# First layer of a two-layer cross-attention kernel: one step of the context's turning ahead of tile 0's scores, three ahead of tile 1's

## The chip, the cores and the metric

The kernel runs on one core of a Trainium2 chip. The metric is the time of one execution in microseconds on the device; the profile beside it is of one other execution. The engines are TensorE (PE; PEld is its weight load), VectorE (DVE), ScalarE (ACT), GpSimd (POOL) and SyncE (SP, which issues most DMAs).

## The reference

Two layers run over x (2048 tokens by 256) and a context of 1601 rows by 192. The change lies in the first layer's attention. Cut to that:

```python
tok = input_tokens @ W_proj + b_proj                      # 1601 x 256
scores = einsum('bnd,bsd->bns', prev_states, tok) / sqrt(D)
attn = softmax(scores, axis=-1)
routed = einsum('bns,bsd->bnd', attn, tok)
# then: layer norms, gates u and r, a candidate, new_state = (1-u)*prev + u*cand, a layer norm
```

The second layer is self-attention with 16 heads, cross-attention to the context with 16 heads, and an MLP. All is float32.

## The kernel before

**First layer.** The scores are not made from `tok` but with the projection folded into the queries: `queries(b)` multiplies 512 tokens of x (turned, `xy_sb`) by `wT_sb`, the turned W_proj, and copies the result back into `xy_sb` on ScalarE (L265). `scores(t)` multiplies 128 tokens (a tile, 16 in all) by the context as it comes from memory, features on the partitions (`ctxA` 128 rows, `ctxB` the other 64, held twice). It writes 1601 scores into two PSUM buffers of 801 and 800, first the product with `ctxA` in four pieces, then the one with `ctxB`. VectorE takes the maximum of each half (L302) and forms the shift (L306, L310), with a bias term that `query_bias(t)` has summed (GpSimd L279, ScalarE L280). ScalarE then writes the exponentials of each half into `pr_xn` (L313). `turned(t)` transposes them in 32x32 blocks on VectorE into `pT` (L320).

**The context's turning.** For the values the context is needed with its rows on the partitions. `turn_context(i0, n)` transposes n blocks of 128 context rows on TensorE, two transposes a block (L331 through the helper at L101, and L333), into one PSUM buffer, and ScalarE copies them out two blocks at a time (L341) into `tok_ctx`, which lies in the places of `pT` that tiles 6 and 7 use later. There are 13 blocks, in four calls: (0,4), (4,4), (8,4) and (12,1). `spread_context` then copies `tok_ctx` by 20 DMAs on SyncE's queue (L352, L356) into `ctx4`, which `mean_context(0)` reads after tile 7.

**What sets the order.** `kept` holds each engine's instructions in the order in which the program names them, so the calls' order in the source is the order on TensorE, VectorE, ScalarE and GpSimd. DMAs on SyncE's queue are ordered by a scheduler. PSUM buffers come from `half()`: four buffers of 2 x 512 floats on 128 partitions, taken in turn; one `queries`, one `turn_context` takes one, `scores` takes two. Whoever takes a buffer waits until its last reader is done with it.

The order around the change is: `queries(0)`, `query_bias(0)`, `scores(0)`, two turning steps, `query_bias(1)`, `scores(1)`, `turned(0)`, the other two steps and the spreading, loads of x, `queries(1)`, and then tiles 2 to 7.

**After that** come the remaining queries, `mean_context(0)`, tiles 8 to 15, projections, `mean_context(1)`, the gates with the second layer's preparation interleaved by a written list (`FIRST`), the long stretch of the second layer's attention, and the MLP.

Of the kernel before, what the change touches and what calls it, by code (L numbers as in the profile page):

```python
# [70 lines left out]
def xattn_kernel(  # L71
# [21 lines left out]
    def kept(ins):  # L93
        tc.keep_in_program_order(ins)
        return ins

    def mm(out_, lhsT, rhs, **kw):
        kept(nc.tensor.matmul(out_, lhsT, rhs, **kw))  # L98

    def transpose(out_, in_):  # L100
        kept(nc.tensor.transpose(out_, in_, ident))  # L101
# [39 lines left out]
    def row(name, p=P):  # L141
        at, w = _ROWS[name]
        t, base = rows_of[at < first_rows]
        return t[:p, at - base : at - base + w]
# [89 lines left out]
    def half():  # L234
        return halves.tile([P, 2, QB], F32, name="half")
# [17 lines left out]
    def queries(b):  # L253
        pt = half()
        for m in range(2):
            for c in range(2):
                mm(
                    pt[:, m, :],
                    wT_sb[:, c, m * P : (m + 1) * P],
                    xy_sb[:, c, b * QB : (b + 1) * QB],  # L260
                    start=(c == 0),
                    stop=(c == 1),
                )
        for m in range(2):
            kept(nc.scalar.copy(xy_sb[:, m, b * QB : (b + 1) * QB], pt[:, m, :]))  # L265
# [10 lines left out]
    def query_bias(t):  # L276

        xb = xbs[t % 2]
        kept(nc.gpsimd.tensor_mul(xb, res[:, t, :], row("b_proj")))  # L279
        kept(nc.scalar.activation(xb, xb, AF.Identity, accum_out=cbs[:, t : t + 1]))  # L280

    def scores(t):
        hs = [half().rearrange("p b n -> p (b n)") for _ in range(2)]
        pieces = [hs[0][:, LEFT:], hs[1][:, : L - H0]]
        outs = [pieces[i // 2][:, n0 - (i // 2) * H0 :][:, :nw] for i, (n0, nw) in enumerate(KEYS)]
        tok = slice(t * P, (t + 1) * P)


        for o, (n0, nw) in zip(outs, KEYS):
            mm(  # L290
                o, xy_sb[:, 0, tok], ctxA[:, n0 : n0 + nw],
                start=True, stop=False, skip_group_check=True,
            )
        for i, (o, (n0, nw)) in enumerate(zip(outs, KEYS)):
            r = slice(i % 2 * (C - P), (i % 2 + 1) * (C - P))
            mm(
                o, xy_sb[r, 1, tok], ctxB[r, n0 : n0 + nw],
                start=False, stop=True, skip_group_check=True,
            )
        nm2 = small.tile([P, 2], F32, name="l0_nm2")  # L300
        for i in range(2):
            kept(nc.vector.tensor_reduce(nm2[:, i : i + 1], pieces[i], AX.X, ALU.max, negate=True))  # L302
        nmx = small.tile([P, 1], F32, name="l0_nmx")
        cb = cbs[:, t : t + 1]
        kept(
            nc.vector.scalar_tensor_tensor(  # L306
                nmx, nm2[:, 0:1], nm2[:, 1:2], cb, ALU.min, ALU.subtract
            )
        )
        kept(nc.vector.tensor_scalar(nmx, nmx, cb, 1.0 / 16.0, ALU.add, ALU.mult))  # L310
        for i, (k0, kw) in enumerate(((0, H0), (H0, L - H0))):
            kept(
                nc.scalar.activation(  # L313
                    pr_xn[:, t % 2, k0 : k0 + kw], pieces[i], AF.Exp, bias=nmx, scale=1.0 / 16.0,
                    accum_out=dens[:, t, i : i + 1],
                )
            )

    def turned(t):
        kept(nc.vector.transpose(pT[:, t % T8, :], pr_xn[:, t % 2, :]))  # L320
# [5 lines left out]
    def turn_context(i0, n):  # L326
        pt = half()
        for i in range(n):
            k0, kw = LC[i0 + i]
            at_i = pt[:kw, i // 2, i % 2 * C : (i % 2 + 1) * C]  # L330
            transpose(at_i[:, :P], ctxA[:, k0 : k0 + kw])  # L331
            kept(
                nc.tensor.transpose(  # L333
                    at_i[:, P:], ctxB[: C - P, k0 : k0 + kw], ident[: C - P, : C - P]
                )
            )
        for b in range(0, n, 2):
            m = min(2, n - b)
            kw = LC[i0 + b][1]
            kept(  # L340
                nc.scalar.copy(  # L341
                    tok_ctx[:kw, i0 + b : i0 + b + m, :],
                    pt[:kw, b // 2, : m * C].rearrange("p (i n) -> p i n", n=C),
                )
            )

    def spread_context():
        for j in range(P // HP):
            r = slice(j * HP, (j + 1) * HP)
            n = (KB - 1 - j) // 4 + 1 if j != (KB - 1) % 4 else (KB - 1) // 4  # L350
            for i in range(P // HP):
                nc.sync.dma_start(ctx4[i * HP : (i + 1) * HP, j::4, :][:, :n, :], tok_ctx[r, :n, :])  # L352
        left = L - (KB - 1) * HP
        j = (KB - 1) % 4
        for i in range(P // HP):
            nc.sync.dma_start(  # L356
                ctx4[i * HP : i * HP + left, KB - 1, :],
                tok_ctx[j * HP : j * HP + left, (KB - 1) // 4, :],
            )
# [96 lines left out]


    queries(0)
    query_bias(0)
    scores(0)  # L460
    turn_context(0, 4)
    turn_context(4, 4)
    query_bias(1)
    scores(1)
    turned(0)
    turn_context(8, 4)
    turn_context(12, 1)
    spread_context()
    for t4 in range(2, 4):
        load_x(t4)  # L470
    queries(1)
# [805 lines left out]
```

## Time and profile before

| what | us |
|---|---|
| median of 3 runs (1918.60 to 1924.24) | 1922.65 |
| the profiled execution's own time | 1927.1 |
| its span | 1925.3 |
| TensorE busy in the span | 1909.5 |
| VectorE busy | 1423.1 |
| ScalarE busy | 1339.0 |
| GpSimd busy | 675.6 |

The span is the part of the execution that the profile's records cover; 1.8 us lie around it. The first layer ends at about 196 us of the span. Mean granted clock of TensorE over the span: 0.996. Lines of the profile below give, for a group of instructions, its start, its duration, the engine, the line of the code, the operation, the tile written and the tiles read, the shape, the count, and in brackets the engine's idle time before it and what ended it.

### The profile page before, as it was taken

To read this page: it belongs to the slowest core of one execution; us is meant where nothing else is said; L and a number is where in the kernel's file an instruction comes from. 1 tells how busy PE (TensorE), PEld (TensorE's weight loads), DVE (VectorE), ACT (ScalarE), POOL (GpSimd) and SP (SyncE) were. 2 spreads that over 40 slices of the span, in tenths; PEclk is the share of its full clock that TensorE was granted. 3 is DMA by queue.
4 is the path that set the end of the run, shared out by engine and by line. 5 is a ranking of instruction groups with operands and counts; after the bars stand their busy time and mean duration, and the time that the engine had idled before them with its cause. 6 is when DMAs were issued, how large, how long until landed. Compare 5 with 4: busy or idle time off the path is not lost.

```text
span 1925.3 us, 39186 instructions
## 1 busy us (share of the span) xinstructions
PE 1909.5 (99%) x14774; PEld 855.0 (44%) x14774; DVE 1423.1 (74%) x2546; ACT 1339.0 (70%) x2598; POOL 675.6 (35%) x850
## 2 busy tenths in 40 slices
PE   8999999999999999999999999999999999999999
PEld 4758775433333333433333344333333433443466
DVE  3563575888888888878888888788888878886210
ACT  3322433188887888788888887887888788888621
POOL 1202334034444444343444444344444344343010
PEclk9999998999999999999999999999999999999999
DMA  7400404500000000000000000000000000000000
GB/s 198 96 32 24 51 1 83 81 3 6 6 5 2 5 5 5 8 5 5 5 5 5 5 5 5 5 7 2 27 26 5 8 5 5 5 5 2 1 22 22
DMA packets 32894, 38.27 MB, mean 20 GB/s; under 512 B 12416, under 2 KB 25088, under 8 KB 32320
## 3 DMA queue, kind: packets, MB, share of 16 engines
q1 hardware_dynamic: 30880, 29.98, 7.3%
q0 software_dynamic: 1168, 4.11, 0.8%
q10 hardware_dynamic: 656, 1.67, 0.6%
q8 instruction: 116, 1.90, 0.4%
q14 instruction: 74, 0.61, 0.1%
HBM read 16.27 MB, written 2.62 MB: 10 GB/s over the span
## 4 chain that ended last, share of the span: by engine, by line
PE 85%; DVE 4%; POOL 1%; DMA 0%; issue 0%; ACT 0%; DVEq 0%; POOLq 0%
PE bank L98 84%; DVE mxp L670 2%; PE bank L101 1%; DMA stage<-in_ca_wq_dram 0%; DVE bn_st L827 0%; DVE bn_st L892 0%; DVE nr_v L178 0%; DVE cand_sb L977 0%; DVE res L978 0%; DVE res L995 0%; POOL ca_wo_sb L537 0%; DVE mvb L828 0%; DVE cand_sb L976 0%; POOL rs_o_a L186 0%; DVE res L990 0%
## 5 line engine op out<-in xcount | busy, mean ns | idle before, releaser
L670 DVE TENSOR_REDUCE mxp<-bank 128x1 f32<-128x512 f32 x1792 | 1109.1, 681 | 171.9 <-PE bank L98 165.4
L716 ACT ACTIVATE pt<-bank 128x512 f32<-128x512 f32 (+1 forms) x1856 | 959.8, 602 | 201.3 <-PE bank L98 200.7
L742 POOL TENSOR_TENSOR acc<-acc,part 128x512 f32<-128x512 f32 x414 | 526.0, 1270 | 840.9 <-ACT part L741 840.9
L98 PE MATMUL bank<-qa,k_sa 32*128 32x512 f32 x2048 | 519.7, 615 | 0.4
L98 PE MATMUL bank<-k_sa,qa 32*128 32x512 f32 x2048 | 504.8, 619 | 0.0
L98 PE MATMUL bank<-k_ca,qa 32*128 32x512 f32 (+1 forms) x2048 | 432.6, 531 | 0.0
L98 PE MATMUL bank<-qa,k_ca 32*128 32x512 f32 (+1 forms) x1664 | 414.9, 617 | 0.0
L98 PEld LDWEIGHTS bank<-qa,k_sa 32*128 32x128 f32 x2048 | 216.5, 183 | 226.4 <-DVE mxp L670 203.6
L98 PE MATMUL bank<-pt,v_sa 128*32 128x512 f32 x2048 | 272.8, 605 | 0.0
L741 ACT COPY part<-bank 128x512 f32<-128x512 f32 x414 | 252.7, 610 | 13.2 <-PE bank L98 10.0
L98 PEld LDWEIGHTS bank<-qa,k_ca 32*128 32x128 f32 (+1 forms) x1664 | 166.4, 179 | 179.6 <-DVE mxp L670 143.5
L98 PEld LDWEIGHTS bank<-k_sa,qa 32*128 32x128 f32 x2048 | 197.5, 184 | 69.6 <-ACT pt L716 44.2
L98 PE MATMUL bank<-pt,v_ca 128*32 128x512 f32 (+1 forms) x1664 | 225.0, 605 | 0.0
L98 PEld LDWEIGHTS bank<-k_ca,qa 32*128 32x128 f32 x2048 | 196.4, 184 | 47.3 <-ACT pt L716 32.7
L98 PEld LDWEIGHTS bank<-pt,v_sa 128*32 128x32 f32 x2048 | 40.3, 108 | 192.1 <-ACT pt L716 191.1
L98 PEld LDWEIGHTS bank<-pt,v_ca 128*32 128x32 f32 (+1 forms) x1664 | 34.7, 108 | 150.6 <-ACT pt L716 148.6
L1195 DVE TENSOR_TENSOR o<-bank,res 128x512 f32<-128x512 f32 (+1 forms) x9 | 5.6, 631 | 97.0 <-PE bank L98 97.0
L98 PE MATMUL half<-l_pT,ctx 32*128 32x256 f32 (+1 forms) x1632 | 71.0, 376 | 2.7 <-DVE routed L418 1.3
L98 PE MATMUL half<-ctx_w,xy_sb 128*128 128x512 f32 (+5 forms) x256 | 71.1, 516 | 1.1 <-ACT xy_sb L265 0.7
L98 PEld LDWEIGHTS half<-l_pT,ctx 32*128 32x128 f32 (+1 forms) x1632 | 65.3, 158 | 8.6 <-issue 3.7
L313 ACT ACTIVATE pr_xn<-half,l_nmx 128x801 f32<-128x801 f32 (+1 forms) x32 | 29.4, 925 | 47.5 <-DVE l_nmx L310 47.5
L302 DVE TENSOR_REDUCE l_nm<-half 128x1 f32<-128x801 f32 (+1 forms) x32 | 30.2, 986 | 34.8 <-PE half L98 34.8
(187 smaller groups left out, 1307.6 us busy)
## 6 DMA issues: line engine op xcount, KB each, us to landing
ctx<-l_pT SPq DMA_DIRECT2D x8, 312.0 KB
ctx<-l_pT SPq DMA_DIRECT2D x8, 288.0 KB
xy_sb<-in_xT_dram SPq DMA_DIRECT2D x4, 512.0 KB
res<-in_x_dram SPq DMA_DIRECT2D x4, 512.0 KB
k_sa<-hT_sa SPq DMA_DIRECT2D x16, 128.0 KB
k_sa<-k SPq DMA_DIRECT2D x64, 32.0 KB
qa<-hT_sa SPq DMA_DIRECT2D x64, 32.0 KB
qa<-hT SPq DMA_DIRECT2D x64, 32.0 KB
```

The source lines that it names most:

```text
L98: kept(nc.tensor.matmul(out_, lhsT, rhs, **kw))
L101: kept(nc.tensor.transpose(out_, in_, ident))
L302: kept(nc.vector.tensor_reduce(nm2[:, i : i + 1], pieces[i], AX.X, ALU.max, negate=True))
L313: nc.scalar.activation(pr_xn[:, t % 2, k0 : k0 + kw], pieces[i], AF.Exp, bias=nmx, scale=1.0 / 16.0, accum_out=dens[:, t, i : i + 1],)
L670: kept(nc.vector.tensor_reduce(mxps[n][:, j, qt, kb : kb + 1], mx, AX.X, ALU.max))
L716: kept(nc.scalar.activation(pt[:kw], sc[:kw], AF.Exp, scale=HD**-0.5))
L741: kept(nc.scalar.copy(part, av))
L742: kept(nc.gpsimd.tensor_add(accs[n], accs[n], part))
L1195: kept(nc.vector.tensor_add(o[:, some, :], po[:, :n, :], res[:, t0 : t0 + n, :]))
```

## The change

`turn_context(0, 4)` is moved from behind `scores(0)` to ahead of `query_bias(0)`. The calls `turn_context(8, 4)`, `turn_context(12, 1)` and `spread_context()` are moved from behind `turned(0)` to ahead of `query_bias(1)`. Nothing else differs: every instruction is issued as often as before.

```diff
     queries(0)
+    turn_context(0, 4)
     query_bias(0)
     scores(0)
-    turn_context(0, 4)
     turn_context(4, 4)
+    turn_context(8, 4)
+    turn_context(12, 1)
+    spread_context()
     query_bias(1)
     scores(1)
     turned(0)
-    turn_context(8, 4)
-    turn_context(12, 1)
-    spread_context()
     for t4 in range(2, 4):
         load_x(t4)
     queries(1)
```

The order of the built programs differs on TensorE, ScalarE and SyncE as the diff says, and nowhere behind `queries(1)` on any engine; of the 16 large copies of `spread_context` the first that is issued is one of 13 blocks where it was one of 12.

## Prediction

> **What bounds the kernel now.** I read the page first (busy time of each engine), then the chain of waits, then TensorE's waits over the whole span, then the timeline of TensorE and ScalarE in the first 40 us, and at the end the stretches with their granted clock.
>
> The page:
>
> ```profile
> span 1925.3 us, 39186 instructions
> PE 1909.5 (99%) x14774; PEld 855.0 (44%) x14774; DVE 1423.1 (74%) x2546; ACT 1339.0 (70%) x2598; POOL 675.6 (35%) x850
> PE 85%; DVE 4%; POOL 1%; DMA 0%; issue 0%; ACT 0%; DVEq 0%; POOLq 0%
> ```
>
> TensorE (PE) has work 1909.5 of 1925.3 us, and 85% of the chain that ended last is TensorE. So a change of order gains at most TensorE's holes, about 16 us in all, and one made ahead of tile 1 reaches only the holes that stand there. TensorE's waits, the first of up to 300 us, the second of from 300 us on:
>
> ```profile
> PE half L98 <- ACT xy_sb L265: 1.2, 2, 0.7
> PE half L98 <- ACT pr_xn L313: 0.9, 1, 0.9
> ...
> PE bank L98 <- DVE v_ca L1046: 2.0, 1, 2.0
> ```
>
> The first has two parts, 0.68 us ahead of tile 0's scores and 0.53 at 71 us. The timeline of TensorE shows where they stand (start, duration, idle before in brackets):
>
> ```profile
> 8.03 6.58 PE L98 MATMUL half<-xy_sb,rows_sb 128*128 128x512 f32 x8 [1.93 <-DMA xy_sb<-in_xT_dram]
> 15.29 4.50 PE L98 MATMUL half<-ctx_w,xy_sb 128*128 128x289 f32 x16 [0.68 <-ACT xy_sb L265]
> 19.72 0.33 PE L101 MATMUL half<-ident,ctx_w 128*128 128x128 f32 x1
> ...
> 23.42 4.51 PE L98 MATMUL half<-ctx_w,xy_sb 128*128 128x289 f32 x16
> 27.86 0.33 PE L101 MATMUL half<-ident,ctx_w 128*128 128x128 f32 x1
> ...
> 29.96 0.27 PE L333 MATMUL half<-ident,ctx_w 64*65 64x64 f32 x1
> 31.10 5.30 PE L98 MATMUL half<-xy_sb,rows_sb 128*128 128x512 f32 x8 [0.88 <-ACT pr_xn L313]
> 36.25 26.58 PE L98 MATMUL half<-ctx_w,xy_sb 128*128 128x289 f32 x96
> 62.75 7.13 PE L98 MATMUL half<-xy_sb,rows_sb 128*128 128x512 f32 x16
> ```
>
> The reader is to see five pieces: queries(0) until 14.61; scores(0) at 15.29; two turning steps 19.72 to 23.42 (3.70 us, 1.85 each); scores(1) 23.42 to 27.86; the last two steps until 30.22, then a hole of 0.88, and queries(1) at 31.10. From 36.25 on TensorE runs without a hole to 69.8. The hole of 0.68 is ScalarE's copy of the queries; that of 0.88 is the PSUM buffer of scores(1)'s first half, which queries(1) takes next and which the exponential (L313) gives back.
>
> queries(1) took 36.25 - 31.10 = 5.15 us, while queries(2) and (3) together took 69.82 - 62.75 = 7.07, 3.54 each. The 1.6 us between are the clock, in the table of stretches (third figure from the end: the share of the clock that was granted; behind it DMA share and GB/s):
>
> ```profile
> 30.00:31.00 1.00, 0.23 (x2) 0.09 (x1) 1.00 (x1) 0.97 (x3) 0.00 (x0) 0.98 0.00 0
> 31.00:32.00 1.00, 0.90 (x1) 0.50 (x2) 0.72 (x1) 1.00 (x4) 0.00 (x0) 0.50 0.00 0
> ...
> 34.00:35.00 1.00, 1.00 (x4) 0.40 (x3) 0.00 (x0) 0.00 (x0) 0.00 (x0) 0.82 0.80 159
> ...
> 315.00:317.00 2.00, 2.00 (x7) 0.95 (x10) 2.00 (x5) 0.92 (x2) 2.00 (x4) 0.50 0.26 57
> ```
>
> Half clock from about 31.0 to 34.4 (3.4 us), and again from about 314.3 (0.82 mean in 313 to 315) to 324.5 (0.62 in 323 to 325), 10.2 us, which cost about half of it, 5.1.
>
> **The change, part by part.** No instruction is added or taken away: 26 transposes, 7 ScalarE copies and 20 DMAs issue as before. turn_context(0,4) moves ahead of scores(0); turn_context(8,4), (12,1) and spread_context move ahead of scores(1).
>
> *Step 1, ahead of scores(0).* The context's rows that it reads are there: SyncE's queue reuses the semaphores of those loads, and its waits for them end at 11.30 and 13.1. It needs no copy of the queries, so it starts when queries(0) ends, at 14.61, and takes 1.85: scores(0) starts at 16.46, not 15.29. The 0.68 hole is filled: 1.85 of work costs 1.17. Its two copies (0.40 us each, from four in 1.62) lie in ScalarE's idle 1.79 us ahead of query_bias(0) at 17.51. Gain 0.68.
>
> *Steps 2 to 4, ahead of scores(1).* With t the start of scores(0), from the same trace: TensorE is done with it at t + 4.43, with two turning steps at t + 8.13, and with the 0.52 of turn_context(12,1) at t + 8.65. The four PSUM buffers are taken in turn, so turn_context(12,1) takes tile 0's first half and scores(1) its second. The exponentials say when these are free:
>
> ```profile
> 21.91 0.93 ACT L313 ACTIVATE pr_xn<-half,l_nmx 128x801 f32<-128x801 f32 x1 [3.88 <-DVE l_nmx L310]
> ...
> 22.82 0.92 ACT L313 ACTIVATE pr_xn<-half,l_nmx 128x800 f32<-128x800 f32 x1
> ...
> 23.73 1.62 ACT L341 COPY l_pT<-half 128x384 f32<-128x384 f32 x4
> ```
>
> The first ends at 22.84, t + 7.55, against t + 8.13: 0.58 to spare. The second ends at 23.74, t + 8.45, against t + 8.65: 0.20 to spare. scores(1)'s second half takes turn_context(4,4)'s buffer, whose two copies stand behind the exponentials and end at about t + 9.3; TensorE gets there a quarter of 4.43 into scores(1), t + 9.75. All three margins hold, the narrowest by 0.2. So TensorE runs on, and behind scores(1), at t + 13.1, queries(1) takes the buffer of turn_context(8,4), emptied by about t + 10.1: today's hole of 0.88 is gone. What could come back instead is bounded by 0 and by a hole like today's, 0.88; I take 0, since each margin is above nothing.
>
> *What is late next.* Tile 0's maximum (L302) and exponentials come 1.2 us later; VectorE idles 5.67 us ahead of tile 1's, and scores(2) takes its second half's buffer from scores(1)'s first exponential, which ends 7.55 behind scores(1)'s start, at t + 16.2, and is wanted at t + 13.1 + 3.54 + 1.1 = t + 17.7. query_bias(1) stands on ScalarE behind five copies (1.9 us), about t + 10.4 to t + 11, and is wanted by tile 1's shift at about t + 15. VectorE and ScalarE keep pace from there as they do now.
>
> *The 20 DMAs.* On SyncE's queue they keep their place behind sa_wk's load of 16.63 and wait for the last copy of the turning, so they start at about 27 and not 32.73. The loads from HBM have ended by then (DMA share 0.23 in 25 to 26, 0.07 in 26 to 27), and issuing took 29.2 us (32.73 to 61.95), so they end near 56. Their readers, and turned(6), which writes over their source, come from 64.99 on and TensorE shows no wait for them at 69.82: nothing to gain, and no cost. The next load on the queue, sa_wv at 76.35, waits for GpSimd in any case.
>
> *Sum.* 0.68 + 0.88 = 1.56 us off the path, and everything behind hangs on TensorE or on steps released by it, so it should reach the end. Against this execution's own time, 1927.1 (span 1925.3 and 1.8 around it): 1925.5 with both cold stretches as they are, 1923.9 without the one at 31. The execution stands 4.45 above the median 1922.65 of the runs (1918.6 to 1924.24); cold stretches of 1.6 and 5.1 are enough for such a difference, so I take the median, with its share of them: 1922.65 - 1.56 = 1921.1.
>
> *The clock.* The stretch that went cold had, since 27.86, transposes alone (2.36 us) and the hole; the longer one at 19.72, 3.70 us, kept its clock at 1.00. After the change transposes run unbroken from t + 4.43 to t + 8.65, 4.22 us. On the one row that would cost 1.6, on the other nothing. I take nothing on balance: one stretch at risk in place of two (3.70, and 3.24 with the hole), but a longer one.
> [...]
>
> **The rivals.** (a) *The clock falls during the unbroken transposes.* For it: the half clock at 31 right behind transposes. Against: 1.00 through 3.70 us of them. It decides in the median once it holds in most executions and lasts over 2 x 1.56 = 3.1 us. One stretch of 3.4: 1922.65 - 1.56 + 1.6 = 1922.7, just slower; as long as at 314, 10.2: 1922.65 - 1.56 + 5.1 = 1926.2, slower.
> (b) *A PSUM wait takes the old one's place*, ahead of scores(1): the margin of 0.20 is used up by the semaphores' way, or the exponentials slip. For it: four buffers, all in use. Against: the margins above. With a hole of 0.88: 1922.65 - 0.68 = 1922.0.
> (c) *The cold stretch at 31 goes and none comes*: its hole is gone, and matmuls follow scores(1) at once. If the median run had it, 1921.1 - 1.6 = 1919.5. Against: the median lies 4.45 under the profiled run, so it need not have had it.
> (d) *It is absorbed*, by the wait for v_ca at 312 (2.0 us), behind the 8.91 us of ca_wq's load: then 1922.65. Against: that load is issued at 291.4, behind steps that hang on TensorE.
>
> **How the numbers follow.** Forecast 0.50, (a) 0.18, (b) 0.13, (c) 0.14, (d) 0.05. Predicted 1921.1. The runs shown lie up to 2.8 on either side of their middle: the low end is (c) less that, 1916.7, the high end (a)'s first value with it, 1925.5; (a)'s long form is left out. What a measurement can tell from no change is 0.3%, 5.8 us; no case's own price reaches it, so faster by that (under 1916.9) is (c) with luck, 0.09, slower (over 1928.4) is (a)'s long form with bad luck, 0.06, and within it 0.85.
>
> **What would show it.** Step 1 right: transposes directly behind queries(0), scores(0) near 16.5 without an idle bracket. Steps 2 to 4 right: no bracket of over 0.1 from there to queries(1), which begins near 29.6, and scores(2) near 33. (a): PEclk under 1.00 between 21 and 29. (b): a bracket <-ACT pr_xn L313 ahead of scores(1). DMAs of L352 near 27. Wrong altogether if the time moves by more than 6 us while these hold: then something behind 36 us changed, which I hold to be shifted alone.

## The result, and the profile after

The changed kernel took 1920.64 us in the median of 20 executions (1916.76 to 1925.95), the kernel before beside it 1924.32 (20 executions, 1918.60 to 1927.49). The ratio is 0.9983, with a 95% interval of 0.9976 to 0.9991: some 3.3 us faster (1.7 to 4.6), at a scatter of 2.2 to 2.5 us from one execution to the next.

The two profiled spans lie 7.3 us apart, 1925.3 and 1918.0, more than twice what the executions say. So the first thing to do with the new profile is not to explain its span, but to sort what the change moved from what differs between any two executions. TensorE's waits of the changed kernel over its whole span (us in total, times, longest):

```profile
PE bank L98 <- DVE v_ca L1046: 1.4, 1, 1.4
...
PE half L333 <- DMA ctx_w<-in_ctxT_dram: 1.0, 1, 1.0
PE half L98 <- ACT xy_sb L265: 0.5, 1, 0.5
```

The wait for the exponentials (pr_xn, 0.88) is gone, and of the two for the copied queries only the 0.53 at 67 us is left: both holes that the prediction named are filled. A new wait stands there, for the context's load. The timeline of TensorE, changed kernel:

```profile
7.72 3.67 PE L98 MATMUL half<-xy_sb,rows_sb 128*128 128x512 f32 x8 [1.62 <-DMA xy_sb<-in_xT_dram]
11.23 0.27 PE L101 MATMUL half<-ident,ctx_w 128*128 128x128 f32 x1
12.47 0.27 PE L333 MATMUL half<-ident,ctx_w 64*128 64x64 f32 x1 [0.96 <-DMA ctx_w<-in_ctxT_dram]
...
14.06 4.50 PE L98 MATMUL half<-ctx_w,xy_sb 128*128 128x289 f32 x16
18.49 0.33 PE L101 MATMUL half<-ident,ctx_w 128*128 128x128 f32 x1
...
22.66 6.20 PE L98 MATMUL half<-ctx_w,xy_sb 128*128 128x289 f32 x16
28.78 3.70 PE L98 MATMUL half<-xy_sb,rows_sb 128*128 128x512 f32 x8
32.32 26.58 PE L98 MATMUL half<-ctx_w,xy_sb 128*128 128x289 f32 x96
```

The reader is to see two things. From 12.47 to 65.9 us no bracket is left. And the same instructions have other lengths than before: queries(0) took 3.67 us where it took 6.58, scores(1) 6.20 where it took 4.51, queries(1) 3.70 where it took 5.30. That is the clock, shown for scores(1) and queries(1) by the stretches of the changed kernel (third figure from the end: granted clock), and for queries(0) inferred from its passes alone (last section):

```profile
22.00:23.00 1.00, 1.00 (x5) 0.68 (x5) 0.00 (x0) 1.00 (x4) 0.00 (x0) 1.00 1.10 350
23.00:24.00 1.00, 1.00 (x3) 0.52 (x2) 0.00 (x0) 1.00 (x4) 0.00 (x0) 0.60 1.10 359
...
26.00:27.00 1.00, 1.00 (x4) 0.38 (x2) 0.00 (x0) 0.00 (x0) 0.00 (x0) 0.70 0.96 162
...
310.00:316.00 6.00, 6.00 (x15) 2.90 (x11) 5.51 (x14) 1.33 (x2) 1.38 (x3) 0.50 0.46 68
```

A mean of 0.60 in the 23rd microsecond and 0.70 in the 26th, with 0.50 between, is half clock for 0.8 + 2 + 0.6 = 3.4 us (23.2 to 26.6 taken alone: 0.50). It now falls on scores(1), where in the profile before it fell on queries(1). Later it is 6.8 us long (0.50 from 309.9 to 316.7), where it was 10.2 (0.50 from 314.3 to 324.5).

From the start of queries(0) to that of scores(2) the profile before has 28.22 us (8.03 to 36.25), the one after 24.60 (7.72 to 32.32). By pieces, start to start: queries(0) with its hole 7.26 and 3.51, of which the hole is 0.68 and the clock 3.07; the turning steps 6.94 (with the hole of 0.88) and 7.00 (with the wait of 0.96); scores(1) 4.44 and 6.12; queries(1) 5.15 and 3.54. Of the 3.62 us only 0.68 + 0.88 - 0.96 = 0.60 are holes; the rest is clock. The other 3.7 us of the two spans come from the start (0.31), two gaps near 102 and 106 us, for which the profile names no wait and which of these two only the profile before has (0.76), and the stretch at 310 us (2.6), where nothing was changed.

### The profile page after: what moved, and what is told of

The parts are those of the page before. It is cut to its first block, busy times and chain, and to the rows that moved or that the text cites. A ratio compares the mean times of both kernels' runs of the same rounds, so it can differ in the third digit from the quotient of the medians.

```text
span 1918.0 us, 39182 instructions
## 1 busy us (share of the span) xinstructions
PE 1904.4 (99%) x14774; PEld 853.5 (44%) x14774; DVE 1423.2 (74%) x2546; ACT 1339.0 (70%) x2598; POOL 675.7 (35%) x850
## 4 chain that ended last, share of the span: by engine, by line
PE 94%; DVE 4%; DMA 1%; POOL 1%; issue 0%; ACT 0%; SPq 0%; DVEq 0%; POOLq 0%
PE bank L98 84%; PE half L98 9%; DVE mxp L670 2%; PE bank L101 1%; DMA ctx_w<-in_ctxT_dram 0%; DMA stage<-in_ca_wq_dram 0%; DVE bn_st L827 0%; DVE bn_st L892 0%; PE half L101 0%; DVE nr_v L178 0%; PE half L333 0%; DVE cand_sb L977 0%; DVE res L978 0%; DVE res L995 0%; POOL ca_wo_sb L537 0%
## 5 line engine op out<-in xcount | busy, mean ns | idle before, releaser
L98 PE MATMUL bank<-hT_sa,k_sa 128*128 128x512 f32 x128 | 55.7, 593 | 0.0
```

## The experiments

The mean granted clock of every execution is recorded beside its time, for the kernel before too in all but the first comparison. That turned out to be the instrument of the study: a mean of 0.997 in place of 0.998 is 3.8 us more of half clock (0.001 x 1920 / 0.5), 1.9 us lost. Executions of the same kernel, by that clock (number of executions, mean us), over all runs below, with the 20 executions of the changed kernel above:

```
clock     before              changed             queries(1) in the middle
0.994     6   1926.17
0.995     16  1924.36         2   1923.72
0.996     18  1923.10         12  1922.55         2   1922.16
0.997     23  1922.77         16  1919.91         12  1919.55
0.998     22  1919.67         10  1918.40         5   1919.21
0.999     16  1919.88         3   1917.01         7   1916.02
1.000     4   1915.99                             3   1915.72
mean      105 at 0.99698      43 at 0.99700       29 at 0.99790
```

"At equal clock" below is a straight line fitted through all 215 executions (these 177 and 38 of the other versions): one offset for each kernel and one slope, which came out at 1.5 us for each 0.001 of clock, where the sum above gives 1.9. The scatter around it is 1.4 us, against 2.5 without the clock. The +/- are standard errors.

**The kernel before, once more** (no edit).

> The kernel before, once more, for a second profile of it and its granted clock in many executions. Theory A (the two filled holes, 0.68 and 0.88 us, are the gain, and cold stretches fall on both kernels alike): ratio 1.000; whether queries(0) runs at full clock changes from execution to execution, and the stretch behind the last turning step is cold in some executions only. Theory B (the measured 3.2 us are the holes and some 1.7 us of half clock that the kernel before has behind the hole ahead of queries(1) in most executions): ratio 1.000, and this profile shows half clock again during queries(1).

1921.05 us (11 executions), ratio 0.9996 (0.9986 to 1.0007). Its profile:

```profile
23.84 6.20 PE L98 MATMUL half<-ctx_w,xy_sb 128*128 128x289 f32 x16
33.22 3.70 PE L98 MATMUL half<-xy_sb,rows_sb 128*128 128x512 f32 x8 [0.88 <-ACT pr_xn L313]
```

The hole of 0.88 is there to the hundredth, but queries(1) behind it ran at full clock (3.70 us), and scores(1) ran cold (6.20). So the same program goes cold in one place or the other. In its third profile, below, both were cold (queries(1) 5.40 us). Theory B stands or falls with the mean clock, then: if the change took a cold stretch away in most executions, its mean would be higher by some 0.0009. The table has 0.99698 and 0.99700, with an error of 0.00015 each: no such rise. Where both kernels ran beside each other with their clocks, in the second and third comparisons below, the changed kernel's mean is higher by 0.0006 and 0.0002, each +/- 0.0004, so a smaller rise is not excluded.

**Step 1 alone.**

```diff
     queries(0)
+    turn_context(0, 4)
     query_bias(0)
     scores(0)
-    turn_context(0, 4)
     turn_context(4, 4)
```

> Only turn_context(0,4) is moved ahead of scores(0); the other steps stay as before. Theory A: 0.7 us faster than before (ratio 0.9996), the bracket of 0.68 ahead of scores(0) gone, the hole of 0.88 ahead of queries(1) still there. Theory B: the same, since the hole ahead of queries(1) and the cold stretch behind it stay.

1921.90 us (11), ratio 0.9993 (0.9984 to 1.0003); at equal clock 0.8 +/- 0.45 us faster, where 0.7 was expected. Its timeline shows scores(0) without a bracket and the other hole as it was:

```profile
7.58 5.23 PE L98 MATMUL half<-xy_sb,rows_sb 128*128 128x512 f32 x8 [1.48 <-DMA xy_sb<-in_xT_dram]
14.43 4.50 PE L98 MATMUL half<-ctx_w,xy_sb 128*128 128x289 f32 x16
20.72 4.57 PE L98 MATMUL half<-ctx_w,xy_sb 128*128 128x289 f32 x16
28.47 3.70 PE L98 MATMUL half<-xy_sb,rows_sb 128*128 128x512 f32 x8 [0.88 <-ACT pr_xn L313]
```

**Steps 2 to 4 alone.**

```diff
     scores(0)
     turn_context(0, 4)
     turn_context(4, 4)
+    turn_context(8, 4)
+    turn_context(12, 1)
+    spread_context()
     query_bias(1)
     scores(1)
     turned(0)
-    turn_context(8, 4)
-    turn_context(12, 1)
-    spread_context()
```

> Only turn_context(8,4), (12,1) and the spreading are moved ahead of scores(1); turn_context(0,4) stays behind scores(0), so all transposes stand in one unbroken stretch of some 6.1 us. Theory A: the hole of 0.88 goes; 0.9 us faster if the clock holds (ratio 0.9995). [...]

1922.90 us (12), ratio 0.9999 (0.9988 to 1.0010), mean clock 0.9960 against 0.9970 of the kernel before beside it. At equal clock it is 0.9 +/- 0.44 us faster (0.88 was the hole); the clock takes that back. The stretches of its profile:

```profile
18.00:22.60 4.60, 4.60 (x22) 2.56 (x19) 2.29 (x4) 2.07 (x5) 0.57 (x1) 0.99 1.07 374
22.60:25.30 2.70, 2.70 (x8) 1.35 (x8) 0.00 (x0) 1.95 (x6) 0.00 (x0) 0.50 1.02 341
25.30:29.40 4.10, 4.10 (x7) 2.19 (x7) 0.00 (x0) 0.89 (x4) 0.73 (x1) 0.51 0.55 100
```

The transposes begin at 18.35; 4.1 us later the clock halves, and it stays so for 6.8 us, through the last transposes and the first 4 us of scores(1). This is rival (a) of the prediction, made to happen. Over the twelve executions it cost 1.5 us (0.0010 of clock), about what the prediction gave one stretch (1.6): a gain gone.

**queries(1) between the second step and the last two.** The changed order, with the transposes broken up.

```diff
     turn_context(4, 4)
+    queries(1)
     turn_context(8, 4)
     turn_context(12, 1)
     spread_context()
     query_bias(1)
     scores(1)
     turned(0)
     for t4 in range(2, 4):
         load_x(t4)
-    queries(1)
```

> The changed order, but queries(1) stands between the second turning step and the last two, so that no stretch of transposes is longer than 2.4 us and no hole is left. [...] If it is no faster than the changed kernel, cold stretches in the first 40 us are not what made the difference.

1918.25 us (12), ratio 0.9981 (0.9969 to 0.9992) where 0.9988 was expected, mean clock 0.9983. Its profile holds full clock from 12.2 to 300 us (its second profile, below, has 3.4 us of half clock near 190 us, its third none there):

```profile
12.20:300.00 287.80, 283.16 (x2466) 204.29 (x2465) 160.94 (x351) 98.02 (x206) 76.83 (x234) 1.00 0.31 68
```

**The changed kernel again.**

> The changed kernel once more, on a chip and beside runs of the kernel before that are new. The mean granted clock of its first 20 executions was 0.9968, that of 35 executions of the kernel before 0.9969, so the clock behind the first matmuls gives it nothing. Theory A (the two holes alone, and the first 3.2 us were partly chance): 1.6 us faster, ratio 0.9992. Theory C (something else in the moved order gives another 1.7 us): ratio 0.9983 again.

1919.51 us (11), ratio 0.9983 (0.9974 to 0.9992): the first ratio again, as Theory C had it. But this time the clocks are known: 0.9970 for the changed kernel, 0.9964 for the kernel before beside it, worth 0.0006 x 1.5 per 0.001 = 0.9 us of the 3.1 between the means. That leaves 2.2, with a standard error of some 0.5, between Theory A's 1.6 and Theory C's 3.3.

**queries(1) in the middle, beside it.**

> The version with queries(1) between the second step and the last two, beside the changed kernel on one chip. Theory A with the clock (holes 1.6 us, and a mean granted clock higher by 0.0013, 2.5 us): 4.1 us faster than before (0.9979) and some 2.5 us faster than the changed kernel. If both come out alike, the higher clock of its first 12 executions was chance.

1917.42 us (5), ratio 0.9967 (0.9955 to 0.9980); the mean is 2.5 +/- 1.1 us under the changed kernel's in the same comparison.

**The long stretch, with matmuls by the identity in place of transposes** (the edit stands on top of steps 2 to 4 alone).

```diff
-            transpose(at_i[:, :P], ctxA[:, k0 : k0 + kw])
-            kept(
-                nc.tensor.transpose(
-                    at_i[:, P:], ctxB[: C - P, k0 : k0 + kw], ident[: C - P, : C - P]
-                )
-            )
+            mm(at_i[:, :P], ctxA[:, k0 : k0 + kw], ident, start=True, stop=True)
+            mm(
+                at_i[:, P:], ctxB[: C - P, k0 : k0 + kw], ident[: C - P, : C - P],
+                start=True, stop=True,
+            )
```

> The order in which all four steps stand in one stretch between scores(0) and scores(1), but each block is turned by an ordinary matmul with the identity in place of a transpose; the context's rows come out the same. [...]

1933.06 us (5), ratio 1.0048 (1.0036 to 1.0061). Expected was a ratio of 0.9992, with a clock that holds. The miss is complete: the clock did not hold, it fell for longer. Timeline and stretches:

```profile
18.84 14.53 PE L98 MATMUL half<-ident,ctx_w 128*128 128x128 f32 x52
33.30 5.91 PE L98 MATMUL half<-ctx_w,xy_sb 128*128 128x289 f32 x16
```

```profile
18.90:22.50 3.60, 3.60 (x21) 2.73 (x20) 1.89 (x4) 1.48 (x3) 0.00 (x0) 1.00 1.06 371
22.50:33.00 10.50, 10.50 (x33) 7.66 (x34) 0.00 (x0) 2.68 (x8) 0.00 (x0) 0.50 0.29 97
33.00:36.00 3.00, 3.00 (x6) 1.69 (x7) 0.00 (x0) 0.97 (x4) 0.72 (x1) 0.50 0.26 45
```

TensorE was busy without a break, with ordinary matmuls, and went to half clock all the same, for 13.7 us. So half clock came here without a single transpose in the stretch.

**The changed order with matmuls by the identity** (the same edit on the changed kernel).

> The changed order with matmuls in place of the transposes. By the holes 1.6 us and by the clock some 0.7 us over the kernel before with its transposes and more: 2 to 4 us faster (0.9979 to 0.9990), mean clock 0.998, no cold stretch between 15 and 300 us in the profile. If matmuls by the identity take longer than transposes (0.46 us a block of 128 rows), the gain is less by 13 times the difference.

1930.56 us (5), ratio 1.0032 (1.0019 to 1.0044), mean clock 0.9956 where 0.998 was expected. The four blocks of the first step take 3.02 us (13.47 to 16.49) where transposes take 1.85, so 13 blocks cost 3.8 us more. It was expected faster and is 6.9 us slower than the kernel before, so 3.8 less the holes' 1.6 are not all of it. Its profile shows half clock for 6.8 us from 26.6 and for 3.4 us near 202, and a gap of 2.46 us at 105.7 for which it names no wait; the two versions with matmuls in one stretch have such a gap too, of 1.36 and 1.89 us. What brings these gaps about was not tried, so the times of the three versions with matmuls say little; their clocks say more.

**The same with dense operands.**

```diff
-            mm(at_i[:, :P], ctxA[:, k0 : k0 + kw], ident, start=True, stop=True)
+            mm(at_i[:, :P], ctxA[:, k0 : k0 + kw], ctxA[:, :P], start=True, stop=True)
             mm(
-                at_i[:, P:], ctxB[: C - P, k0 : k0 + kw], ident[: C - P, : C - P],
+                at_i[:, P:], ctxB[: C - P, k0 : k0 + kw], ctxB[: C - P, : C - P],
```

> The order of the one long stretch, with matmuls whose second operand is the first 128 rows of the context and not the identity, so the turned context is replaced by products of the context with itself; all else runs as before. It asks what the clock goes by in the stretch that ran at half clock for 13.7 us with the identity. If it goes by the operands' content (an identity is nearly all zeros): full clock in the stretch, 26 short matmuls at 0.19 us a pass in 10 us. If it goes by how short the matmuls are (128 columns to a weight load): half clock again for 10 us or more, the time as with the identity, ratio 1.005.

1930.36 us (5), ratio 1.0047 (1.0025 to 1.0069). The stretches:

```profile
18.90:22.50 3.60, 3.60 (x21) 2.70 (x19) 1.97 (x4) 1.39 (x3) 0.41 (x1) 1.00 1.06 375
22.50:33.00 10.50, 10.50 (x35) 7.72 (x34) 0.00 (x0) 2.83 (x8) 0.00 (x0) 0.51 0.33 109
33.00:36.00 3.00, 3.00 (x6) 1.62 (x7) 0.00 (x0) 0.90 (x4) 0.72 (x1) 0.50 0.28 49
```

Half clock again for 13.7 us: it is not the zeros. What these three cold stretches have in common is short passes, 64 or 128 columns behind each weight load. The weight load is busy 7.7 of the 10.5 us here. That the shortness is the cause is not shown: no run turns the same blocks in longer passes. In the matmuls of scores(1), behind them, the clock came back at about 36 us (0.92 from 36 to 39 us, and 0.97 with the identity).

**Third comparison: the changed kernel, the kernel before, and queries(1) in the middle.**

> The changed kernel beside the kernel before on one chip, both with their granted clock per execution. Over the executions so far, at equal clock, the changed kernel is 1.6 to 2.0 us faster, and the mean clock of both is the same (0.9969). Theory A (the holes, 1.56 us, and the clock by chance): 1.6 us faster at equal clock, and the plain ratio off from 0.9992 only by what the two mean clocks differ. Theory C (another 1.7 us): 3.2 us faster at equal clock.

1918.98 us (12), ratio 0.9991 (0.9978 to 1.0005), mean clock 0.9973. Against all 44 executions of the kernel before in this comparison (1921.35, clock 0.9972) its mean is 2.1 us lower, and a line fitted through this comparison alone gives 1.9 +/- 0.47 at equal clock: Theory A's 1.6 fits, Theory C's 3.2 does not.

> The kernel before, for more executions with their clock beside the changed kernel's. Ratio 1.000 by every theory.

1920.77 us (12), ratio 0.9998 (0.9985 to 1.0012). Its profile has both holes again (0.68 and 0.88), and queries(1) cold behind the second.

> The version with queries(1) in the middle, beside both. By the holes and the clock: 2.5 us faster than the changed kernel, 4 us faster than before (0.9979); the mean clock 0.998 again, against 0.997 of both.

1919.16 us (12), ratio 0.9992 (0.9980 to 1.0004): no faster than the changed kernel here, and its mean clock only 0.9975. Its three comparisons give 0.9981, 0.9967 and 0.9992 against the kernel before, the third not clear of 1, and over all of them it is 2.1 +/- 0.31 us faster at equal clock, so it beats that one. Whether it beats the changed kernel stays open: 2.5 +/- 1.1 us faster in one comparison, 0.2 +/- 0.8 in the other.

## Why the prediction was right, and where its size was off

The forecast was 1921.1 us and a gain of 1.56; measured were 1920.64 and, by the ratio, 3.3. That the time came out within 0.5 us is in part luck: the forecast starts from a median of three, 1922.65, and the 20 executions of the kernel before have 1924.32, from which 1.56 would lead to 1922.8. What holds is the mechanism, both holes filled, and at equal clock its size. Point by point:

- *Step 1.* The hole ahead of scores(0) is filled, in every profile of that order. Alone it was worth 0.8 +/- 0.45 at equal clock, for 0.68. What failed is the sentence that the context's rows "are there": that held in the profiles in which queries(0) took 5.2 us or more and ended at 12.6 or later. In three profiles of kernels with step 1, the changed kernel's first and third and one with queries(1) in the middle, queries(0) took 3.67 us, and the step waited 0.96 to 1.43 us for the context's load. In the third profile of the changed kernel scores(0) behind that wait then ran at half clock (0.50 from 13.6 to 20.4 us). The prediction saw one execution, and took its slow queries(0) for the rule. No profile with the old order has queries(0) at 3.67 us, so what step 1 is worth in such an execution is not shown.
- *Steps 2 to 4.* All three PSUM margins held. With t = 14.06 the first exponential ended at 21.61 (t + 7.55) against 22.19, the second at 22.51 (t + 8.45) against 22.66, a margin of 0.15 where 0.20 was worked out. Alone the steps were worth 0.9 +/- 0.44 at equal clock, for 0.88. Rival (b) did not come in any profile of an order with steps 2 to 4 moved.
- *The 20 DMAs.* They began at 24.34, t + 10.3, as worked out, and nothing waited for them. That their earlier start is worth nothing was not tried by itself.
- *The sum.* At equal clock the changed kernel is 1.6 +/- 0.26 us faster over all executions, and 1.9 +/- 0.35 if each comparison is given its own level: the term of 1.56 is right within its error, and both parts alone add up to it (0.8 + 0.9).
- *The clock*, "I take nothing on balance", is the term that a single comparison can upset. Over all executions it is indeed nothing (0.99698 before, 0.99700 after), and the profiles agree: behind queries(0) and ahead of scores(2) the three of the kernel before have half clock for 3.4, 3.4 and 6.8 us, the three of the changed kernel for 3.4, 3.4 and 6.8 us as well. But it is not nothing within one comparison: in the second, 0.9 us of 3.1 were the clock's. In the first, where the ratio comes from, the clocks of the kernel before were not recorded, so its surplus of 1.7 us over 1.56 is not accounted for. The mean clock may also leave out a cold queries(0): the last section has the inference. How long queries(0) runs cold and the wait near 310 us are candidates; neither was shown to differ between the kernels. (Its 3.67 us stand in three of eight profiles with step 1 and in none of six without, but the order up to queries(0) is the same in all, and so few can fall that way by chance.)
- *Rival (a)* happened in the changed kernel's own first profile (scores(1) 6.20 us), and in the second of the kernel before as well: the risk is on both sides, as the prediction weighed it. What the clock goes by, no run shows. Where the stretch was made longer (some 6.1 us at full clock), it ate the gain.

## What to carry to other kernels

When a change is worth 0.1%, two profiles can't show it: these two differed by 7.3 us, of which the holes made 0.6. Compare piece by piece from start to start, take out what ran at another clock, and put the mean granted clock beside every timed execution; it took the scatter here from 2.5 to 1.4 us. Filling TensorE's holes with short work has a price that no busy figure shows: in these profiles half clock came within or behind stretches of some 3 to 4 us of transposes, waits among them included, or of matmuls of 128 columns, but not behind each of them (3.70 us held in the first profile of the kernel before and not in its second; 4.16 us held in the third of the changed kernel and 4.17 not in its first). In the three profiles with queries(1) in the middle, where no unbroken stretch is longer than 2.3 us, none came ahead of 180 us once queries(0) was done. So spread such work between long matmuls.

## What the runs showed of the hardware that was not expected

- The stretches of half clock (0.50) lasted 3.4 us (23.2 to 26.6 after the change), 6.8 (steps 2 to 4 alone), 10.2 (314.3 to 324.5 in the profile before), and 13.7 with the short matmuls: near one, two, three and four times 3.4. Why they have these lengths is not shown. Matmuls of 128 columns went cold as transposes did: 0.50 and 0.51 from 22.5 to 33 us.
- The start of this kernel ran at different speeds without the profile's clock saying so each time: queries(0) took 6.58, 5.37 or 3.67 us in different profiles of the same eight passes. Where it took 5.37, 3.4 us of half clock are on record within it. In the profile before, its 6.58 us stand in stretches shown at 1.00, but its weight loads start 0.85 us apart, where those of the 3.67 us start 0.43 apart. That this is half clock is inferred from the factor of two.
- The largest swing lies where nothing was changed. TensorE waits once near 310 us for v_ca, behind a load of ca_wq that took 7.0 to 8.9 us to land. In the eleven profiles with transposes the wait was 1.1 to 1.2 us three times, and the clock stayed at 1.00; it was 1.3 to 2.0 us eight times, and half clock followed for 6.8 or 10.2 us. Half of that, 3.4 to 5.1 us, is lost by the clock (an estimate from the 0.50), and it goes with the landing of one transfer: 7.0 to 7.1 us to landing went with waits of 1.1 to 1.3, 7.3 with 1.4, 7.5 with 1.6, and 7.9 to 8.9 with 1.9 to 2.0. Why the landing differs is not shown. A third place lies between 189 and 197 us, where TensorE waits 1.93 us in each of these profiles and turns eight blocks behind it: 3.4 us of half clock followed in two of the eleven. The kernel before in its second profile, TensorE's waits from 300 us on and the stretch from 300 to 330 us at full clock:

```profile
PE bank L98 <- DVE v_ca L1046: 1.2, 1, 1.2
```

```profile
300.00:330.00 30.00, 28.76 (x117) 14.93 (x115) 18.48 (x44) 12.63 (x22) 13.32 (x42) 1.00 0.34 58
```
